# Causal masks of sixteen small heads: from four products of 64x128 to one corner in spare rows and four products of 64x64

## The chip, the cores and the metric

The kernel runs on one core of one Trainium2 chip, in one launch. The metric is the device time in microseconds (us) of that core; the figure compared is the median over several executions. Before the change three executions took 657.17, 661.19 and 665.92 us, so the median is 661.19 us. The profile is of another, single execution, which took 661.49 us; its span from the first to the last instruction of the program is 659.3 us, and the 2.2 us between the two lie around the span.

## The reference, cut to what matters

The input is x of 8 sequences of 512 tokens with 128 features. Two sublayers are added to it, each between layer norms. The first is attention with one wide head of 128. The second starts with attention of 16 heads of width 4 and goes on with a mixture of 8 experts, 2 of which serve a token. The change touches only the 16 small heads:

```python
L, H = (64, 16); HD = L // H                       # 16 heads, 4 wide
h = _rmsnorm(x, g1); c = h @ w_down
q = _rope(split(c @ wq), pos); k = _rope(split(c @ wk), pos); v = split(c @ wv)
scores = jnp.einsum('bhqd,bhkd->bhqk', q, k) / jnp.sqrt(jnp.float32(HD))
causal = jnp.tril(jnp.ones((s, s), bool))          # s = 512 here
scores = jnp.where(causal, scores, -jnp.inf)
attn = jax.nn.softmax(scores, axis=-1)
o = jnp.einsum('bhqk,bhkd->bhqd', attn, v)
```

A query must not see a key behind it. In blocks of 128 queries and 128 keys only the block on the diagonal needs a mask; the blocks above it are left out of the work, and those below it are whole.

## The kernel before, in words

**Stages.** In the first some 120 us the wide attention of all 8 sequences runs (`wide_attention`). From 93 us the small heads run, as 32 units: 8 sequences by 4 groups of 4 heads (`Unit`). From 467 us the experts run (`experts`), and the last results are written.

**How the heads lie.** Each float of a query or a key is split into three bf16 parts, and the products of the parts that matter make 36 rows (`S9`) on the partitions. Two heads, called i = 0 and 1, lie on partitions 0 to 63 and 64 to 127 of `q_rows` and `k_rows` (`HR` is 64). Of the 64 rows of a head, 0 to 35 are the parts, 36 to 61 are zeros, and 62 and 63 (`SM` is 62) are ones in `k_rows` and the negative row maximum in `q_rows`, which L703 writes by DMA. The constant rows are written once, in `fill` (L161), by DMAs from the tile `fixed`.

**A unit.** The scores are computed twice. `rowwise` (L654) puts queries on the partitions, for a block t of 128 queries and the keys up to it, in tile `sm`; `highest` (L674) lets the VectorE (DVE) take the maximum of each row, tile `nm`, L678. `columnwise` (L710) puts keys on the partitions, for a block j of keys and the queries from it on, in tile `sT`; `weights` (L731) lets the ScalarE (ACT) take the exponent, tile `pk`, L741. `weigh` (L743) then multiplies with the values: products of 128 rows and 32 columns, four side by side, into `po`, L748. `sm` and `sT` share three PSUM buffers with everything else that is called "wide", so the TensorE (PE) can start a new group only when DVE or ACT has read the group three before it.

**A group and its masks.** A group is the score products of one or two pairs of heads (L663 in `rowwise`, L718 in `columnwise`: each with 62 or 64 contracted rows and 128 output partitions, for i = 0 and i = 1 in the two halves of the rows) and then the mask, added to the diagonal blocks by `mask` (L642): for each i and for each half h of the block's columns, a product of a 64x128 mask tile with a 64x64 identity adds 0 or -2^100 to all 128 partitions by 64 columns (L646). These are four products for one pair, or four with twice the columns for two pairs. In a unit there are six row groups (four with one pair, two with two) and five column groups (two with one pair, three with two). That makes 352 groups and 1,408 mask products.

**Order.** `period(n)` (L1283) is an order written out by hand: `both` issues a row group of the unit two ahead, then a column group of this unit, then the reductions and exponents of both, and `weigh` products between them. `aside` (L1268) puts pieces of other work between the steps: `ffn_front` and `ffn_back` (projections, transposes) and `route` (the choice of experts). Each engine executes its own instructions in program order. The constant tiles are made on GpSimd (POOL): `mask_q` and `mask_k` by `half_masks` (L436), called from `late_constants` in the first step of the wide attention; `fixed` in `fill`, three steps later.

Of the kernel before, what the change touches and what calls it, by code (L numbers as in the profile page):

```python
# [9 lines left out]
BF16 = mybir.dt.bfloat16  # L10
I32 = mybir.dt.int32
AF = mybir.ActivationFunctionType
ALU = mybir.AluOpType
AX = mybir.AxisListType

P = 128
EPS = 1e-5

NEG_BF = -(2.0**100)
# [3 lines left out]
def kernel(  # L23
# [22 lines left out]
    nc = tc.nc  # L46
    B, T, D = x.shape
    NT = T // P
    L = w_down.shape[1]
    H, HD, HP = 16, 4, 32  # L50
    NG = H // 4
    HR, S9 = P // 2, 9 * HD
    SM = HR - 2
# [8 lines left out]
    const = ctx.enter_context(tc.tile_pool(name="const", bufs=1))  # L62
# [27 lines left out]
    for b in range(B):  # L90
        nc.sync.dma_start(
            out=x_all[:, b * NT : (b + 1) * NT, :],
            in_=x[b].rearrange("(t p) d -> p t d", p=P),
# [33 lines left out]
    for s in range(2):  # L127
# [3 lines left out]
        for c in range(FC):  # L131
            nc.sync.dma_start(
                out=wall[:, es, 2 * F + c * D : 2 * F + (c + 1) * D],
                in_=w2[es, c * P : (c + 1) * P].rearrange("e f d -> f e d"),
# [14 lines left out]
    q_rows, k_rows = [], []  # L149
    for i in range(2):  # L150
        q_rows.append(during.tile([P, H // 2, T], BF16, name=f"q_rows{i}"))
        rows = during.tile([P, H // 2, T], BF16, name=f"k_rows{i}")
# [8 lines left out]
    def fill():  # L161
        for i, pad in enumerate(vpads):
            nc.gpsimd.memset(pad, 0.0)
            nc.gpsimd.memset(pad[:, :, :, i * 2 * HD + HD : i * 2 * HD + HD + 1], 1.0)
            yield
        fixed = const.tile([P // 2, 1, T], BF16, name="fixed")
        nc.gpsimd.memset(fixed[: P // 4], 1.0)
        nc.gpsimd.memset(fixed[P // 4 :], 0.0)
        for rows in k_rows:
            for h in range(2):  # L170
                at = h * HR + SM
                nc.sync.dma_start(
                    out=rows[at : at + 2], in_=fixed[:2].to_broadcast([2, H // 2, T])
                )
        for rows in q_rows + k_rows:
            for h in range(2):
                at = h * HR + S9
                nc.sync.dma_start(
                    out=rows[at : at + SM - S9],
                    in_=fixed[P // 4 : P // 4 + SM - S9].to_broadcast([SM - S9, H // 2, T]),  # L180
                )
        yield

    h_all = keep.tile([P, B * NT, RW], F32, name="h_all")
# [226 lines left out]
    with tc.manual_schedule():  # L411
# [15 lines left out]
        out=mask_a,  # L427
        in_=mask_a,
        compare_op=ALU.is_ge,
        fill=NEG_BF,  # L430
        base=0,
        pattern=[[-1, P]],
        channel_multiplier=1,
    )

    def half_masks(m, sign):  # L436


        nc.gpsimd.memset(m, 0.0)
        for i in range(2):  # L440
            for h in range(2):
                at = m[i * HR : (i + 1) * HR, h, :]
                nc.gpsimd.affine_select(
                    out=at,
                    in_=at,
                    compare_op=ALU.is_ge,
                    fill=NEG_BF,
                    base=sign * HR * h,
                    pattern=[[-sign, P]],
                    channel_multiplier=sign,  # L450
                )

    mask_q = const.tile([P, 2, P], BF16, name="mask_q")
    mask_k = const.tile([P, 2, P], BF16, name="mask_k")
    order = const.tile([P, E], F32, name="order")
    zeros = const.tile([P, RW], F32, name="zeros")
    ones_bf = const.tile([P, P], BF16, name="ones_bf")
# [3 lines left out]
    back_place = const.tile([P, B, 2, NT], I32, name="back_place")  # L461

    def late_constants():
        half_masks(mask_q, -1)
        half_masks(mask_k, 1)
        for e in range(E):
            nc.gpsimd.memset(order[:, e : e + 1], float(E - e))
        nc.gpsimd.memset(zeros, 0.0)
        nc.gpsimd.memset(zeros[:, D : D + 1].bitcast(I32), FAR)
        nc.gpsimd.memset(ones_bf, 1.0)  # L470
        nc.gpsimd.affine_select(
            out=before_me,
            in_=ones_bf,
            compare_op=ALU.is_gt,
            fill=0.0,
            base=0,
            pattern=[[1, P]],
            channel_multiplier=-1,
        )
        nc.gpsimd.memset(upto_me, 1.0)  # L480
        nc.gpsimd.affine_select(
            out=upto_me,
            in_=upto_me,
            compare_op=ALU.is_ge,
            fill=0.0,
            base=0,
            pattern=[[1, E], [-1, E]],
            channel_multiplier=0,
        )
        nc.gpsimd.iota(  # L490
            tile_at,
            pattern=[[P, tile_at.shape[1]]],
            base=0,
            channel_multiplier=0,
            allow_small_or_imprecise_dtypes=True,
        )
        for part in parts:
            part.constants()
# [126 lines left out]
    class Unit:  # L625
# [16 lines left out]
        def mask(self, out, which, i):  # L642

            at = slice(i * HR, (i + 1) * HR)
            for h in range(2):
                nc.tensor.matmul(  # L646
                    out[:, :, h * HR : (h + 1) * HR],
                    which[at, h, :],
                    ident_bf[at, at].unsqueeze(1).to_broadcast([HR, out.shape[1], HR]),
                    start=False,  # L650
                    stop=(h == 1),
                )

        def rowwise(self, t, pairs):  # L654
# [683 lines left out]
    def wide_attention():  # L1338
        for b in range(B + 1):
# [11 lines left out]
            if b == 0:  # L1351
                late_constants()
# [32 lines left out]

    CLOSED = 3
    setup = [prepare(), fill()]
    first = [front_and_rows(0)]
    units_begin = [period(-2), period(-1)]
# [172 lines left out]
```

## Time and profile before

| what | us or share |
|---|---|
| median of three executions | 661.19 |
| the profiled execution, and its span | 661.49, 659.3 |
| stretch of the small heads, 93 to 467 | 374 |
| PE busy in it | 312.69 |
| DVE busy in it; of that the reductions at L678 | 270.91; 194.79 |
| ACT busy in it | 229.71 |
| PE busy with the mask products (L646) in it | 94.54 |
| mean granted TensorE clock, whole span | 0.927 |

A row of groups in the profile gives the line of the kernel, the engine, the operation, the tiles (out<-in), the shape and the count; then the busy time, the mean duration of one, and the idle time before it with what ended it. For PE the shape begins with the rows and columns of the array that the product takes: 64*128 is 64 contracted rows by 128 output partitions, 128*32 is 128 by 32. The moving operand follows: 64x64 bf16 is 64 partitions by 64 columns. PE products are pipelined: a product's duration runs on after the next one has begun, so the busy times of PE say how long something was in flight, and the times from start to start say what a product costs the stream. A timeline merges neighbours of one kind into one line with a count.

### The profile page before, as it was taken

What the parts mean: (1) busy time and instruction counts of PE and PEld (TensorE: products, weight loads), DVE (VectorE), ACT (ScalarE), POOL (GpSimd) and SP (SyncE); (2) the same over time, 40 slices, a digit from 0 to 9 for tenths busy, and PEclk for the clock granted to TensorE, in tenths of its full rate; (3) what the DMA queues carried; (4) which work ended last, traced back from release to release, by engine and by line L of the source; (5) the groups of instructions that cost most, each with busy time, mean ns of one, the idle gap of its engine ahead of it and who ended that gap; (6) DMA issues with size and microseconds to landing.
All of it is one profiled execution on the core that took longest, in us unless ns stands there. A gap on an engine that the chain in (4) does not pass through costs nothing. (4 is left out here: it accounts for less than half of the span.)

```text
span 659.3 us, 14317 instructions
## 1 busy us (share of the span) xinstructions
PE 531.6 (81%) x5098; PEld 313.6 (48%) x5098; DVE 414.7 (63%) x1011; ACT 365.8 (55%) x717; POOL 280.5 (43%) x414
## 2 busy tenths in 40 slices
PE   4999979888989987888989586858889857999810
PEld 2666746544444543434445233424466635666600
DVE  3567846779889888766887474854333514335765
ACT  2656533356768675756776254647755523445642
POOL 3945733122141514653118332050166574555851
PEclk9999989889999999979999597989989987999955
DMA  7741230502312123123241240011411222324453
GB/s 192 199 88 22 60 84 13 134 2 59 90 26 76 49 75 82 51 83 73 54 103 31 66 125 18 3 34 44 106 53 44 73 70 68 83 68 121 127 144 99
DMA packets 65845, 49.36 MB, mean 75 GB/s; under 512 B 10055, under 2 KB 63563, under 8 KB 65776
## 3 DMA queue, kind: packets, MB, share of 16 engines
q1 hardware_dynamic: 58992, 39.03, 23.4%
q0 software_dynamic: 4544, 8.50, 4.0%
q10 hardware_dynamic: 2240, 0.92, 0.5%
q8 instruction: 41, 0.67, 0.4%
q14 instruction: 28, 0.23, 0.1%
HBM read 25.16 MB, written 22.15 MB: 72 GB/s over the span
## 5 line engine op out<-in xcount | busy, mean ns | idle before, releaser
L678 DVE TENSOR_REDUCE nm<-sm 128x2 f32<-128x1024 f32 (+2 forms) x192 | 194.8, 1042 | 57.8 <-PE sm L646 25.2
L741 ACT ACTIVATE pk<-sT 128x1024 f32<-128x1024 f32 x160 | 162.0, 1025 | 98.1 <-PE sT L646 82.5
L814 POOL DMA_INDIRECT answers<-ye_e,xs_e x78 | 78.4, 1006 | 55.8 <-DVE ye_e L1201 37.1
L748 PE MATMUL po<-pk,vpad 128*32 128x512 f32 (+3 forms) x1024 | 100.1, 456 | 2.4 <-ACT foT L933 2.4
L663 PE MATMUL sm<-k_rows,q_rows 62*128 62x256 bf16 (+3 forms) x512 | 73.4, 313 | 23.1 <-DVE nm L678 8.2
L1157 PE MATMUL ph_e<-wall,xT_e 128*128 x156 | 77.7, 621 | 9.0 <-ACT xT_e L1151 7.3
L718 PE MATMUL sT<-q_rows,k_rows 64*128 64x384 bf16 (+3 forms) x512 | 67.0, 309 | 22.0 <-DVE nm L678 11.0
L1169 ACT ACTIVATE sil_e<-ph_e,xs_e 128x256 f32<-128x256 f32 x78 | 32.7, 469 | 68.5 <-PE ph_e L1157 32.2
L1173 DVE TENSOR_TENSOR hid_e<-sil_e,ph_e 128x512 f32<-128x512 f32 (+1 forms) x40 | 27.0, 674 | 60.1 <-ACT sil_e L1169 52.0
L663 PEld LDWEIGHTS <-q_rows 62*128 62x128 bf16 x512 | 25.3, 95 | 72.8 <-issue 66.1
L801 POOL DMA_INDIRECT rows_dram<-h_all,slots x32 | 32.2, 1008 | 60.3 <-DVE slots L1107 52.7
L646 PE MATMUL sm<-ident_bf,mask_q 64*128 64x64 bf16 (+1 forms) x768 | 51.3, 204 | 1.7 <-issue 1.7
L1191 PE MATMUL py_e<-wall,hT_e 128*128 x312 | 44.0, 286 | 7.1 <-DVE ye_e L1201 7.1
L718 PEld LDWEIGHTS <-k_rows 64*128 64x128 bf16 x512 | 24.3, 95 | 51.5 <-issue 48.9
L646 PEld LDWEIGHTS <-mask_q 64*128 64x128 bf16 x768 | 39.9, 98 | 16.4 <-issue 4.1
L646 PE MATMUL sT<-ident_bf,mask_k 64*128 64x128 bf16 (+1 forms) x640 | 44.5, 210 | 0.0
L1191 PEld LDWEIGHTS py_e<-wall,hT_e 128*128 128x128 f32 x312 | 39.8, 199 | 8.2 <-DVE ye_e L1201 7.3
L1201 DVE TENSOR_SCALAR ye_e<-py_e,xs_e 128x128 f32<-128x128 f32 x78 | 23.8, 346 | 30.3 <-PE py_e L1191 12.2
L1157 PEld LDWEIGHTS ph_e<-wall,xT_e 128*128 128x128 f32 x156 | 27.3, 196 | 30.5 <-issue 21.6
L646 PEld LDWEIGHTS <-mask_k 64*128 64x128 bf16 x640 | 31.6, 97 | 12.9 <-issue 1.7
L801 POOL DMA_INDIRECT rows_dram<-rows,slots x32 | 31.1, 972 | 9.8 <-issue 9.2
L286 PE MATMUL pq<-xnT,wqk 128*128 128x512 f32 x64 | 32.1, 628 | 1.8 <-ACT xnT L280 1.2
(205 smaller groups left out, 893.4 us busy)
## 6 DMA issues: line engine op xcount, KB each, us to landing
xs_e<-rows_dram SPq DMA_DIRECT2D x78, 65.5 KB
q_dram<-thirds SPq DMA_DIRECT2D x24, 192.0 KB
k_dram<-thirds SPq DMA_DIRECT2D x24, 192.0 KB
q_rows<-q_dram SPq DMA_DIRECT2D x16, 288.0 KB
k_rows<-k_dram SPq DMA_DIRECT2D x16, 288.0 KB
y<-answers SPq DMA_DIRECT2D x12, 256.0 KB
x_all<-in_L_attn_x_dram SPq DMA_DIRECT2D x8, 256.0 KB
wall<-in_L_ffn_w_dram SPq DMA_DIRECT2D x4, 512.0 KB
```

Of the source, the lines that this page charges most:

```text
L286: nc.tensor.matmul(pq[:, s, :], wqk[:, i, s, :], self.xnT, start=True, stop=True)
L646: nc.tensor.matmul(out[:, :, h * HR : (h + 1) * HR], which[at, h, :], ident_bf[at, at].unsqueeze(1).to_broadcast([HR, out.shape[1], HR]), ...
L663: nc.tensor.matmul(sc[:, i, c * n : (c + 1) * n], self.q[at, 2 * self.g + pair, t * P : n], self.k[at, 2 * self.g + pair, :n], start=(c == 0),
L678: nc.vector.tensor_reduce(self.nm[:, :, pairs[0] : pairs[0] + w, t], sc[:, :, : w * n].rearrange("p i (c n) -> p i c n", n=n), AX.X, ALU.m ...
L718: nc.tensor.matmul(sc[:, i, c : c + n], self.k[at, 2 * self.g + pair, j * P : (j + 1) * P], self.q[at, 2 * self.g + pair, j * P :], start= ...
L741: nc.scalar.activation(p[:, :, :c], sc[:, :, :c], AF.Exp, scale=HD**-0.5)
L748: nc.tensor.matmul(po[h * HP : (h + 1) * HP, j * P :], vpads[self.g][:, j, h, :], self.p[j, h // 2][:, h % 2, :], start=(self.g == 0 and j ...
L801: nc.gpsimd.indirect_dma_start(out=self.rows[:, :], out_offset=bass.IndirectOffsetOnAxis(ap=index, axis=0), in_=src, in_offset=None, bound ...
L814: nc.gpsimd.indirect_dma_start(out=self.answers[:, :], out_offset=bass.IndirectOffsetOnAxis(ap=index, axis=0), in_=src, in_offset=None, bo ...
L1157: nc.tensor.matmul(ph[q][:, i, :], xT[q][:, i * P : (i + 1) * P], part.weights(i0 + i, 0, 2 * F), start=True, stop=True,)
L1169: nc.scalar.activation(sil[:, i], ph[q][:, i, :F], AF.Silu, scale=xs[q][:, i, D + 2 :])
L1191: nc.tensor.matmul(ps[:, i, :], hT[q][:, i, c, :], part.weights(i0 + i, 2 * F + c * D, D), start=(c == 0), stop=(c == FC - 1),)
```

## The change

The mask of a diagonal block of 128 by 128 is taken apart into three corners. The upper right corner, first 64 queries against last 64 keys, is wholly masked: it moves into four of the zero rows of `q_rows` and `k_rows`, one for each block of 128 tokens. Row t of the queries holds 1 at the first 64 tokens of block t, row t of the keys holds -2^100 at its last 64 tokens, so that the score products themselves add -2^100 there. The score products keep their 62 or 64 rows. What is left are the two triangles of 64 by 64 on the diagonal: `mask` adds each by a product of 64 rows by 64 columns into its own quarter, for h = 0 on output partitions 0 to 63 and for h = 1 on 64 to 127. The number of mask products, and the columns that each moves, stay. `mask_q` and `mask_k` shrink to 64 columns; a small tile `marks` is made on POOL in `fill`, and `fill` issues 16 DMAs for the rows 36 to 61 in place of 8. The order of the instructions on PE, DVE and ACT stays the same one by one.

```diff
+        marks = const.tile([NT, 2, T], BF16, name="marks")
+        for k, value in enumerate((1.0, NEG_BF)):
+            nc.gpsimd.memset(marks[:, k], value)
+            for base, sign in ((-HR * k, 1), (HR * (k + 1) - 1, -1)):
+                nc.gpsimd.affine_select(
+                    out=marks[:, k], in_=marks[:, k], compare_op=ALU.is_ge, fill=0.0,
+                    base=base, pattern=[[sign, T]], channel_multiplier=-sign * P,
+                )
-        for rows in q_rows + k_rows:
-            for h in range(2):
-                at = h * HR + S9
-                nc.sync.dma_start(
-                    out=rows[at : at + SM - S9],
-                    in_=fixed[P // 4 : P // 4 + SM - S9].to_broadcast([SM - S9, H // 2, T]),
-                )
+        for k, both in enumerate((q_rows, k_rows)):
+            for rows in both:
+                for h in range(2):
+                    at = h * HR + S9
+                    nc.sync.dma_start(
+                        out=rows[at : at + NT],
+                        in_=marks[:, k : k + 1, :].to_broadcast([NT, H // 2, T]),
+                    )
+                    nc.sync.dma_start(
+                        out=rows[at + NT : h * HR + SM],
+                        in_=fixed[P // 4 : P // 4 + SM - S9 - NT].to_broadcast(
+                            [SM - S9 - NT, H // 2, T]
+                        ),
+                    )
...
-    def half_masks(m, sign):
+    def corner_mask(m, sign):
         nc.gpsimd.memset(m, 0.0)
         for i in range(2):
-            for h in range(2):
-                at = m[i * HR : (i + 1) * HR, h, :]
-                nc.gpsimd.affine_select(
-                    out=at, in_=at, compare_op=ALU.is_ge, fill=NEG_BF,
-                    base=sign * HR * h, pattern=[[-sign, P]], channel_multiplier=sign,
-                )
+            at = m[i * HR : (i + 1) * HR, :]
+            nc.gpsimd.affine_select(
+                out=at, in_=at, compare_op=ALU.is_ge, fill=NEG_BF,
+                base=0, pattern=[[-sign, HR]], channel_multiplier=sign,
+            )
-    mask_q = const.tile([P, 2, P], BF16, name="mask_q")
-    mask_k = const.tile([P, 2, P], BF16, name="mask_k")
+    mask_q = const.tile([P, HR], BF16, name="mask_q")
+    mask_k = const.tile([P, HR], BF16, name="mask_k")
...
             for h in range(2):
+                corner = slice(h * HR, (h + 1) * HR)
                 nc.tensor.matmul(
-                    out[:, :, h * HR : (h + 1) * HR],
-                    which[at, h, :],
+                    out[corner, :, corner],
+                    which[at, :],
                     ident_bf[at, at].unsqueeze(1).to_broadcast([HR, out.shape[1], HR]),
                     start=False,
-                    stop=(h == 1),
+                    stop=True,
                 )
```

More of the change, by code (lines that the diff above doesn't have):

```diff
@@ L174, in fill @@
                 )
-        for rows in q_rows + k_rows:
-            for h in range(2):
-                at = h * HR + S9
-                nc.sync.dma_start(
-                    out=rows[at : at + SM - S9],
-                    in_=fixed[P // 4 : P // 4 + SM - S9].to_broadcast([SM - S9, H // 2, T]),
-                )
+        marks = const.tile([NT, 2, T], BF16, name="marks")
[3 more added lines that the diff above has]
+                nc.gpsimd.affine_select(
+                    out=marks[:, k],
+                    in_=marks[:, k],
+                    compare_op=ALU.is_ge,
+                    fill=0.0,
+                    base=base,
+                    pattern=[[sign, T]],
+                    channel_multiplier=-sign * P,
+                )
+        for k, both in enumerate((q_rows, k_rows)):
[12 more added lines that the diff above has]
+                    )
         yield
@@ L434 @@
     )
-    def half_masks(m, sign):
+    def corner_mask(m, sign):
         nc.gpsimd.memset(m, 0.0)
         for i in range(2):
-            for h in range(2):
-                at = m[i * HR : (i + 1) * HR, h, :]
-                nc.gpsimd.affine_select(
[L444 to L450, printed above, removed]
-                )
-    mask_q = const.tile([P, 2, P], BF16, name="mask_q")
-    mask_k = const.tile([P, 2, P], BF16, name="mask_k")
+            at = m[i * HR : (i + 1) * HR, :]
+            nc.gpsimd.affine_select(
+                out=at,
+                in_=at,
+                compare_op=ALU.is_ge,
+                fill=NEG_BF,
+                base=0,
+                pattern=[[-sign, HR]],
+                channel_multiplier=sign,
+            )
+    mask_q = const.tile([P, HR], BF16, name="mask_q")
+    mask_k = const.tile([P, HR], BF16, name="mask_k")
     order = const.tile([P, E], F32, name="order")
@@ L463, in late_constants @@
     def late_constants():
-        half_masks(mask_q, -1)
-        half_masks(mask_k, 1)
+        corner_mask(mask_q, -1)
+        corner_mask(mask_k, 1)
         for e in range(E):
```

## The prediction

> **What bounds the kernel now.** I read the page's busy shares and slices first, then one stretch from 93 to 467 us, where all the mask products lie, then who waits for whom in it, and last single groups in the timeline. From the page:
>
> ```profile
> PE 531.6 (81%) x5098; PEld 313.6 (48%) x5098; DVE 414.7 (63%) x1011; ACT 365.8 (55%) x717; POOL 280.5 (43%) x414
> ...
> PE   4999979888989987888989586858889857999810
> DVE  3567846779889888766887474854333514335765
> ```
>
> From the table of stretches (columns: length; busy us and count of PE, weight loads, DVE, ACT, POOL; clock; DMA) and from the waits of that stretch (us in total, times, longest):
>
> ```profile
> 93.00:467.00 374.00, 312.69 (x3965) 168.60 (x3964) 270.91 (x534) 229.71 (x384) 118.75 (x177) 0.94 0.23 58
> ...
> PE sT L718 <- DVE nm L678: 11.0, 20, 1.1
> PE sm L663 <- DVE nm L678: 8.2, 18, 2.2
> PE sm L663 <- ACT pk L741: 6.9, 13, 2.4
> PE sT L718 <- ACT pk L741: 4.5, 4, 2.0
> ...
> ACT pk L741 <- PE sT L646: 82.5, 90, 6.9
> DVE nm L678 <- PE sm L646: 25.2, 37, 3.8
> ```
>
> PE is the fullest engine at 84% of the stretch, but DVE has 72%, and PE waits 30.6 us for buffers that DVE or ACT must read first. Of the 352 groups a consumer stands idle for at least 127 (90 + 37). So PE and its readers take turns. I followed the releases back from the last `po` product at 466.9 us, as the page's chain does from the end: of 374 us PE has 184, DVE 123, ACT 24, and 182 of 372 runs of mask records (some groups are split by waits) lie on the chain: half.
>
> What a mask costs is not its 191 to 224 ns of duration, but the time until the next product starts. Timeline (start, length):
>
> ```profile
> 301.07 0.22 PE L646 MATMUL sm<-ident_bf,mask_q 64*128 64x64 bf16 x4
> 301.23 0.23 PE L695 MATMUL m3T_ps<-ident_bf,m 128*32 128x128 bf16 x1
> ...
> 303.48 0.22 PE L646 MATMUL sm<-ident_bf,mask_q 64*128 64x64 bf16 x4
> 303.54 0.38 PE L718 MATMUL sT<-q_rows,k_rows 64*128 64x512 bf16 x2
> 303.75 0.22 PE L646 MATMUL sT<-ident_bf,mask_k 64*128 64x64 bf16 x4
> 303.90 0.43 PE L748 MATMUL po<-pk,vpad 128*32 128x128 f32 x8
> ...
> 309.91 0.29 PE L646 MATMUL sT<-ident_bf,mask_k 64*128 64x128 bf16 x4
> 310.13 0.64 PE L748 MATMUL po<-pk,vpad 128*32 128x256 f32 x8
> ```
>
> Four mask products of 64 columns, followed by a product of the same shape (64*128), take 0.06 us of the stream (303.48 to 303.54). Followed by another shape they take 0.16 (301.07 to 301.23) or 0.15. A change of shape thus costs 0.09 to 0.10 us. The single records agree: from start to start 117 against 26 ns after 64 bf16 columns, 525 against 429 after 512 f32 columns. It doesn't take a change of rows: a 128*32 product of 128 f32 columns is followed by a 128*128 one after 203 ns, where 110 is the step without a change. With 128 columns the masks take 0.22 less one change, 0.12. All masks together: 192 groups x 0.06 + 160 x 0.12 = 30.7 us of stream, not the 94.5 us of busy time.
>
> **The change, part by part.** (1) *Masks in 64*64 instead of 64*128.* In the order of the built program every group now goes from 64*128 to 64*64 (352 changes), and 168 of them go back to 64*128 afterwards; the other 184 were followed by another shape already. The changes of shape rise from 402 to 922, by 520. No row shows 64*128 to 64*64. From below: nothing, since two neighbours named 128*128 and 128*64 cost nothing (112 and 109 ns at 478.8 and 479.2 us, where 110 is the plain step). From above: 98 ns, the dearest ordinary change (128*32 to 64*128). I take 93 ns, because in the built program those 128*64 transposes carry no column group and so are no change, while the new masks carry one, as 128*32 does. 520 x 0.093 = 48.4 us.
>
> (2) *Four quarters at once.* Products of 128*32 start 7 ns apart and run side by side; if quarters do that, a group takes 27 ns of columns (53 for two pairs; 64 and 128 columns at the 0.42 ns that 512 columns in 215 ns give) + 3 x 7 + the weights. The weights can no longer be loaded ahead of the change: 27 ns uncovered for 128*32 f32 (454 from one round of four to the next, for 427 of columns) and 11 for 64*128 bf16 (226 against 215); 64 bf16 columns lie between, or at twice 27 at worst; I take 20. That is 68 and 94 ns against 62 and 118: 192 x 6 - 160 x 24 = -2.7 us. Ends: -17 us (27 and 53 ns with nothing else) and +9 (weights 54).
>
> (3) *Weights after the 168 returns:* 168 x 11 ns = 1.8 us, by the 64*128 row, between 0 and 4.5 (27 ns each).
>
> (4) *Score products:* same rows, columns and count: nothing. DVE and ACT do the same.
>
> (5) *Setup.* POOL makes `marks` after `fixed`, at 36.8 us: two memsets at the 0.51 of `fixed` and four selects of 512 elements, between 0.29 (128 elements, L443) and 1.14 (four times that); at 0.75, 4.0 us together. POOL is idle for 1.64 us before `roped` at 38.40, again for 0.52 us, and after 42.6 us, so the second `roped`, done at 41.46, slips to about 43.3; the scores that read it start at 43.34. Cost 0 to 1 us. If that cover were gone, at most the 4.0. The smaller masks save some 1.5 us on POOL at 18 to 21 us, which can be worth that or nothing; together I put 0. SP issues 8 more DMAs of about 1 us each (L178: 3.85 for four) and starts them up to 4 us later, so it ends near 61 instead of 48.9; what is queued behind is the first `q_dram` store, at 74.42.
>
> Sum on PE: 48.4 - 2.7 + 1.8 = **+47.5 us** of stream in 374 us.
>
> **How much reaches the end.** At most all of it. At least what lies on the chain: half of the entries, (32.7 - 2.7) x 0.49 = 14.7, and 79 of 188 returns by the records, 17.4 x 0.42 = 7.3: 22 us. Each group that becomes later pulls the chain over to PE, so the truth lies between; what hides the rest is DVE's queue of reductions (194.8 us at L678), and without that cover it is 47.5. I take +33, a little under the middle. What is late next is the reader: `nm` and `pk` wait longer for their groups, and the 30.6 us that PE waits for buffers shrink. The experts after 467 us only start later. From the profiled execution 661.49 + 33 = 694.5; the median is 0.3 lower: **694 us**.
>
> The Trainium skill, in "TensorEngine Tiling (Array Packing)", section "Tiling Modes", says that a change of the tiling mode, not of the tile, makes TensorE run empty; the 0.09 to 0.10 us above agree with it, but it has no figure for them. The same page, under "Theoretical Speedup", gives twofold for a small output dimension; by that alone the 30.7 us would halve, an estimate of -15 us, or 646. The section "Gotcha 2: Feature Incompatibilities" there rules out the fast weight load with column tiling, which speaks for the dearer end of (2); no row shows 64 bf16 columns.
>
> **The rivals.** *A: a change between 64*128 and 64*64 costs nothing.* The rows keep their halves, only the columns split in two, and the only changes seen that cost are to or from quarters of the columns or of the row split. For it: the two 128*64 neighbours. Against: 128*32 to 128*128. Price: weights are then loaded ahead, groups take 48 and 74 ns against 62 and 118, 192 x 14 + 160 x 44 = 9.7 us less stream, two thirds of it at the end: 655 us, not slower. It decides below 19 ns a change (520 x 0.019 = 9.7). With the -17 of (2), all on the path, 644.
>
> *B: paid, but hidden.* DVE is busy when 155 of 192 groups arrive, by the waits; if its queue covers two thirds and more of the 47.5, the time is 661.5 + 12 = 673 or less. Against it: 90 of 160 exponents find ACT idle, and the chain's half is a floor.
>
> *C: more than the sum.* Seven pieces of the stretch, 48 us of 374, run at a granted clock of 0.5; there a change costs twice: 520 x 48/374 x 0.093 = 6 us more. With all of the sum on the path: 715. Above that, if the thinner stream is granted the full clock less often.
>
> **How the numbers follow.** Forecast, the changes paid and half to wholly on the path: 0.79, 675 to 715. A: 0.08, of which 0.03 under 648. B: 0.08, 661 to 674. C beyond 716: 0.05. The range 670 to 716 takes in the forecast and the upper part of B, some 8 in 10. This kernel's three runs differ by 1.3%, so under 2% nothing can be told: faster by over 2% (under 648) 0.03, within 2% (to 674.4) 0.13, slower 0.84.
>
> **What would show it.** Masks as 64*64; from the start of the scores to the masks 0.09 us more than the columns take (0.21 at 303.54 to 0.31); from the masks to a score product 0.15 to 0.18 us instead of 0.06; busy time of L646 lower though the stretch is longer; more idle time of DVE and ACT before `nm` and `pk`; POOL and SP unchanged after 75 us. Steps of 0.21 and 0.05 instead would prove A. I am wrong in the price if the stretch grows by over 50 us, in the landing if the steps are as said and it grows by under 15.

## The result

The changed kernel takes 687.61 us (median of four executions, 686.91 to 689.59), the kernel before 659.18 (four, the three named above among them, 654.85 to 665.92): 1.042 times as long, with a 95% interval of 1.037 to 1.047, or 28 us more. The forecast was 694 in a range of 670 to 716. The profiled execution took 686.91 us with a span of 684.8, which is 25.5 us more than the span before.

From the page of the kernel after: busy time of each engine, the busy tenths of PE and DVE in 40 slices, and the shares of the chain that ended last.

```profile
PE 574.3 (84%) x5098; PEld 304.7 (44%) x5098; DVE 417.1 (61%) x1011; ACT 369.2 (54%) x717; POOL 283.1 (41%) x416
...
PE   5999979799999998979989885987979986999910
DVE  3577836768778787756688473676133443434865
...
PE 66%; DVE 14%; ACT 6%; DMA 4%; issue 3%; another core or an unknown queue 3%; POOL 2%; SPq 1%; ACTq 0%; POOLq 0%; DVEq 0%
```

PE is fuller and DVE emptier than before, with as many instructions on each. From the stretch of the small heads, now 93 to 497 us: its row in the table of stretches (columns as before the change), the same for the mask products alone (L666 is the old L646), and the waits (us in total, times, longest).

```profile
93.00:497.00 404.00, 358.03 (x3972) 161.06 (x3970) 272.38 (x536) 233.29 (x386) 118.77 (x177) 0.91 0.21 54
...
93.00:497.00 404.00, 85.70 (x1408) 40.76 (x1408) 0.91 0.21 54
```

```profile
ACT pk L761 <- PE sT L666: 106.9, 103, 5.0
DVE nm L698 <- PE sm L666: 51.7, 57, 4.9
PE sT L738 <- DVE nm L698: 13.2, 24, 4.4
...
PE sm L683 <- ACT pk L761: 5.2, 12, 1.5
...
PE sT L738 <- ACT pk L761: 3.8, 3, 2.6
...
PE sm L683 <- DVE nm L698: 2.1, 4, 0.7
```

The mask products are in flight for less time than before (85.7 against 94.5 us), and yet the stretch is 28 us longer. The readers wait more for the masks: ACT 106.9 us against 82.5, DVE 51.7 against 25.2. PE waits less for buffers: 13.2 + 5.2 + 3.8 + 2.1 = 24.3 us against 30.6. From the first score product to the first transpose of the experts it was 375.7 us (91.6 to 467.2); now it is 403.8 (92.5 to 496.3). So the whole loss lies here; the experts behind it took 192.1 us to the end of the span and now take 188.5, by instructions that the change does not touch, and why they take less is not known.

The timeline of the changed kernel (start, length), at the same place in the order as the lines shown before the change:

```profile
318.49 0.39 PE L683 MATMUL sm<-k_rows,q_rows 62*128 62x512 bf16 x2
318.81 0.22 PE L666 MATMUL sm<-ident_bf,mask_q 64*64 64x64 bf16 x4
318.96 0.23 PE L715 MATMUL m3T_ps<-ident_bf,m 128*32 128x128 bf16 x1
...
321.04 0.34 PE L683 MATMUL sm<-k_rows,q_rows 62*128 62x384 bf16 x2
321.30 0.22 PE L666 MATMUL sm<-ident_bf,mask_q 64*64 64x64 bf16 x4
321.46 0.39 PE L738 MATMUL sT<-q_rows,k_rows 64*128 64x512 bf16 x2
321.78 0.22 PE L666 MATMUL sT<-ident_bf,mask_k 64*64 64x64 bf16 x4
321.93 0.42 PE L768 MATMUL po<-pk,vpad 128*32 128x128 f32 x8
```

From the scores to their masks it is 0.32 us after 512 columns (318.49 to 318.81, 321.46 to 321.78), where it was 0.21 (303.54 to 303.75). From the masks to scores it is 0.16 us (321.30 to 321.46), where it was 0.06. From the masks to a product of another shape it is 0.15 us, as before. The two steps that grew are those at which a change of shape was added.

### The profile page after: what moved, and what is told of

It is laid out like the page before. It is cut to its first block, busy times and chain, and to the rows that moved or that the text cites. A ratio compares the mean times of both kernels' runs of the same rounds, so it can differ in the third digit from the quotient of the medians.

```text
span 684.8 us, 14324 instructions
## 1 busy us (share of the span) xinstructions
PE 574.3 (84%) x5098; PEld 304.7 (44%) x5098; DVE 417.1 (61%) x1011; ACT 369.2 (54%) x717; POOL 283.1 (41%) x416
## 4 chain that ended last, share of the span: by engine, by line
PE 66%; DVE 14%; ACT 6%; DMA 4%; issue 3%; another core or an unknown queue 3%; POOL 2%; SPq 1%; ACTq 0%; POOLq 0%; DVEq 0%
PE po L768 12%; PE ph_e L1177 10%; PE sT L738 7%; PE sm L683 6%; DVE nm L698 6%; PE py_e L1211 5%; PE sm L666 4%; PE sT L666 4%; PE pqk L597 2%; PE pq L306 2%; PE ht_e L1200 2%; ACT pk L761 1%; PE pu L983 1%; PE pr L371 1%
## 5 line engine op out<-in xcount | busy, mean ns | idle before, releaser
L698 DVE TENSOR_REDUCE nm<-sm 128x2 f32<-128x1024 f32 (+2 forms) x192 | 195.1, 1044 | 77.6 <-PE sm L666 51.7
L761 ACT ACTIVATE pk<-sT 128x1024 f32<-128x1024 f32 x160 | 163.5, 1026 | 126.5 <-PE sT L666 106.9
L768 PE MATMUL po<-pk,vpad 128*32 128x512 f32 (+3 forms) x1024 | 102.4, 478 | 1.6 <-ACT foT L953 1.6
L834 POOL DMA_INDIRECT answers<-ye_e,xs_e x78 | 78.9, 1011 | 51.7 <-DVE ye_e L1221 35.0
L738 PE MATMUL sT<-q_rows,k_rows 64*128 64x384 bf16 (+3 forms) x512 | 68.3, 321 | 23.5 <-DVE nm L698 13.2
L1177 PE MATMUL ph_e<-wall,xT_e 128*128 x156 | 76.1, 610 | 8.0 <-issue 4.1
L683 PEld LDWEIGHTS <-q_rows 62*128 62x128 bf16 x512 | 22.1, 94 | 65.0 <-issue 54.7
L666 PE MATMUL sm<-ident_bf,mask_q 64*64 64x64 bf16 (+1 forms) x768 | 45.8, 227 | 0.4 <-issue 0.4
L738 PEld LDWEIGHTS <-k_rows 64*128 64x128 bf16 x512 | 20.7, 95 | 54.1 <-issue 43.6
L666 PEld LDWEIGHTS <-mask_q 64*64 64x64 bf16 x768 | 22.2, 105 | 41.8 <-issue 38.8
L666 PE MATMUL sT<-ident_bf,mask_k 64*64 64x128 bf16 (+1 forms) x640 | 39.9, 236 | 0.8 <-issue 0.8
L666 PEld LDWEIGHTS <-mask_k 64*64 64x64 bf16 x640 | 18.6, 105 | 39.9 <-issue 39.8
```

The lines of the kernel that those rows point to most:

```text
L666: nc.tensor.matmul(out[corner, :, corner], which[at, :], ident_bf[at, at].unsqueeze(1).to_broadcast([HR, out.shape[1], HR]), start=False, ...
L683: nc.tensor.matmul(sc[:, i, c * n : (c + 1) * n], self.q[at, 2 * self.g + pair, t * P : n], self.k[at, 2 * self.g + pair, :n], start=(c == 0),
L698: nc.vector.tensor_reduce(self.nm[:, :, pairs[0] : pairs[0] + w, t], sc[:, :, : w * n].rearrange("p i (c n) -> p i c n", n=n), AX.X, ALU.m ...
L738: nc.tensor.matmul(sc[:, i, c : c + n], self.k[at, 2 * self.g + pair, j * P : (j + 1) * P], self.q[at, 2 * self.g + pair, j * P :], start= ...
L761: nc.scalar.activation(p[:, :, :c], sc[:, :, :c], AF.Exp, scale=HD**-0.5)
L768: nc.tensor.matmul(po[h * HP : (h + 1) * HP, j * P :], vpads[self.g][:, j, h, :], self.p[j, h // 2][:, h % 2, :], start=(self.g == 0 and j ...
```

## The experiments

The runs were made on several chips. On two of them the kernel before takes 609 to 610 us, on a third 660. Every ratio below is to the kernel before on the same chip; the us follow from ratio and that time. In short diffs, "-" is the kernel named in the sentence ahead of it, and "..." stands for lines that are left out.

### The rows alone

The changed kernel with the masks of the kernel before: the corner rows and all their setup stay (`marks` lies in a working tile here), the mask products and their mask tiles are 64x128 again.

```diff
...
-                    out[corner, :, corner],
-                    which[at, :],
+                    out[:, :, h * HR : (h + 1) * HR],
+                    which[at, h, :],
...
```

> The corner rows and their setup as after the change, but the masks as before it: two 64x128 products for each i. No change of shape is added (402 as before). Theory 'changes of shape': nothing of the 27 us is left, 0.995 to 1.01 of the kernel before. Rival 'rows and setup' (marks on GpSimd, 8 more DMAs, rows that are no longer zero): most of the 27 us stays, 1.03 or more.

Measured: 1.0007 (0.998 to 1.003). The marks on GpSimd, the 8 additional DMAs, and rows that hold marks instead of zeros cost nothing that can be told (the interval reaches 1.5 us to either side).

### The quarters alone

The kernel before with the 64x64 masks, but without the corner rows; so the upper right corner of each diagonal block is left unmasked.

```diff
...
-                    out[:, :, h * HR : (h + 1) * HR],
-                    which[at, h, :],
+                    out[corner, :, corner],
+                    which[at, :],
...
```

> The masks as after the change (64x64 products, 922 changes of shape), but the rows 36 to 61 all zero as before it; the masking of the upper right corner of each diagonal block is left out. Theory 'changes of shape': the whole loss is here, 1.035 to 1.05 of the kernel before. Rival 'rows and setup': 1.00 to 1.01.

Measured: 1.0445 (1.039 to 1.050), 27 us. The whole loss is in the shape of the mask products.

### The price of a change of shape by itself

The kernel before with one small product between the scores and the masks of each group. It adds zeros, moves 16 columns, and has 64 output columns in the one run and 128 in the other:

```diff
+            nc.tensor.matmul(
+                sc[:64, 0, :16], no_mask[:HR, :64], ident_bf[:HR, :16],   # or [:128] and [:HR, :128]
+                start=False, stop=False,
+            )
```

> The kernel before, with one small product of 64 rows by 64 columns and 16 moving columns, which adds zeros, between the scores and the masks of each group: 352 products, 704 more changes of shape (352 there, 352 back). Theory 'changes of shape', at 0.09 us each and some 0.03 us for the weights: 352 x 0.21 = 74 us of stream, of which 60 to 90% reach the end, 44 to 67 us: 1.065 to 1.10. Rival 'the quarters and their weights are slow, not the change': 352 x 0.03 to 0.05 = 11 to 18 us of stream, 1.01 to 1.03.

> The same with the small product at 64 rows by 128 columns, the shape of its neighbours: 352 products, no more changes of shape. Theory 'changes of shape': 352 x 0.01 to 0.03 = 4 to 10 us of stream, 1.00 to 1.01. Rival 'any extra product between scores and masks costs so much': as much as with 64x64, 1.06 or more.

Measured: 1.087 (1.083 to 1.091) with 64x64, 53 us; 1.005 (1.003 to 1.008) with 64x128, 3 us. The timeline of the 64x64 run (the small product is L658, the masks L648):

```profile
300.59 0.39 PE L675 MATMUL sm<-k_rows,q_rows 62*128 62x512 bf16 x2
300.91 0.19 PE L658 MATMUL sm<-ident_bf,no_mask 64*64 64x16 bf16 x1
301.04 0.23 PE L648 MATMUL sm<-ident_bf,mask_q 64*128 64x64 bf16 x4
301.11 0.39 PE L731 MATMUL sT<-q_rows,k_rows 64*128 64x256 bf16 x4
```

And of the 64x128 run:

```profile
300.45 0.34 PE L675 MATMUL sm<-k_rows,q_rows 62*128 62x384 bf16 x2
300.63 0.17 PE L658 MATMUL sm<-ident_bf,no_mask 64*128 64x16 bf16 x1
300.63 0.24 PE L648 MATMUL sm<-ident_bf,mask_q 64*128 64x64 bf16 x4
```

With 64x64 the product of 16 columns (7 ns at 0.42 ns each) holds the stream for 0.13 us until the masks, and the masks of four products behind it take 0.07, where it was 0.06. With 64x128 it vanishes between its neighbours. In the single records 347 of the 352 steps from it to the masks are 125 or 126 ns: 7 for the columns, 92 or 93 for the change as on the way in, and some 26 left, which are put down to weights that could not be loaded ahead; no run separates these from the change. So it is neither the number of products nor their columns, but the change of shape: 704 more changes, 352 x 0.22 = 77 us of stream, of which 53 reach the end, 69%. The granted clock plays no part in this one: the profiled execution has 10 us at half clock in the stretch of the small heads, as the run with the rows alone has.

### Fewer changes of shape by another order

The changed kernel with the scores of the row group and of the column group first, and the masks of both behind them:

```diff
...
-                v.rowwise(t, pairs)
+                late.append(v.rowwise(t, pairs))      # scores now, masks later
             for job in between:
                 job()
             if unit:
-                unit.columnwise(parts)
+                late.append(unit.columnwise(parts))
+            for masks in late:
+                masks()
```

> The kernel after the change, but in each call of both the scores of the row group and of the column group come first and the masks of the two last, so that the 64x64 products stand together: 653 changes of shape instead of 922 (402 before the change). Theory 'changes of shape': 251 more than before at 0.09 us = 23 us, less 5 us for the narrower masks of groups with two pairs, times 0.6 = 11 us: 1.01 to 1.025 of the kernel before. Rival 'the 64x64 products themselves are slow': as after the change, 1.04. It can also be slower than the sum says, because the row maxima wait for the column scores too.

Measured: 1.088 (1.083 to 1.093), twice the loss of the change itself. Both theories missed it. The warning at the end of the expectation names what the waits show (`nm` is L702 here, `sT` L742, `pk` L769):

```profile
ACT pk L769 <- PE sT L666: 115.0, 128, 4.0
DVE nm L702 <- PE sT L666: 53.2, 78, 1.9
PE sT L742 <- ACT pk L769: 24.6, 29, 1.0
DVE nm L702 <- PE sm L666: 21.3, 25, 4.3
PE sT L742 <- DVE nm L702: 18.5, 29, 0.8
```

DVE now waits 53.2 us until the column masks are through (0.5 in the run with the rows alone), and PE waits 43.1 us (24.6 + 18.5) for a buffer before the column scores, with the row masks held up behind it. The same order with the masks and the rows of the kernel before separates order and shape.

> The order of the run with the masks together (scores of the row group and of the column group first, then the masks of the two), but with the 64x128 masks and the rows of the kernel before: no change of shape is added (402). Theory 'the order cost that run its gain: the row maxima and the buffers wait for the column scores': this order alone costs 30 to 45 us, 1.05 to 1.075 of the kernel before. Rival '64x64 products that stand together are slow in a way of their own': 1.00 to 1.02.

Measured: 1.061 (1.053 to 1.069), 40 us, without one more change of shape. So the order alone costs 6.1%. If the two losses add up, 2.7% are left for the 251 changes that the first run has above the kernel before, 16 us with some 6 either way, as the two runs were made on different chips; the sum in the expectation had 11 for them. Both runs had a lower granted clock than the kernel before (0.923 to 0.935 against 0.954 to 0.970, and 0.894 to 0.916 against a median of 0.934), so a part of both losses goes with the clock.

### What hides the rest

Two runs, before and after, in which DVE takes the maximum over the first half of the keys only, with the scale of the exponents at 0.05; both give another output than the reference.

```diff
-                sc[:, :, : w * n].rearrange("p i (c n) -> p i c n", n=n),
+                sc[:, :, : w * n].rearrange("p i (c n) -> p i c n", n=n)[:, :, :, : n // 2],
...
-            nc.scalar.activation(p[:, :, :c], sc[:, :, :c], AF.Exp, scale=HD**-0.5)
+            nc.scalar.activation(p[:, :, :c], sc[:, :, :c], AF.Exp, scale=0.05)
```

> The kernel before, with the VectorE taking each row maximum over the first half of the keys only, and the scale of the exponents set to 0.05 so that nothing overflows: the reductions lose some 80 of 195 us of the VectorE's time, and the output is another one. It is the base for the next run. If half of the chain ran through the VectorE, as read from the trace before, 0.93 to 0.97 of the kernel before; if the TensorE alone bounded, 0.99 to 1.00.

> The kernel after the change with the same halved maxima and the same scale of the exponents as the run before it. Theory 'the queue of reductions hides the rest of the 44 us': with a lighter VectorE more of the stream reaches the end, 34 to 44 us above the run before it (0.055 to 0.07 in the ratio). Rival 'it is hidden elsewhere (ScalarE, copies, DMA)': the same 25 to 28 us as with the whole maxima.

Measured: 0.961 (0.957 to 0.965) for the kernel before with halved maxima, 1.013 (1.008 to 1.019) for the kernel after. A row of the groups of each (the kernel before first: busy time, mean ns, idle before):

```profile
L678 DVE TENSOR_REDUCE nm<-sm 128x2 f32<-128x512 f32 (+2 forms) x192 | 112.4, 600 | 73.7 <-PE sm L646 71.5 <-PE sT L646 1.2
```

```profile
L698 DVE TENSOR_REDUCE nm<-sm 128x2 f32<-128x512 f32 (+2 forms) x192 | 113.2, 601 | 100.5 <-PE sm L666 99.6 <-issue 0.7
```

82 us less of DVE (194.8 to 112.4) bring 24 us, so DVE did carry a part of the path before. The change of the masks now costs 0.052 of 609.9, 32 us, against the 27 of the quarters with whole maxima. That lies between what the two theories expected (34 to 44, and 25 to 28), and with the intervals of the ratios (some 4 us each way on the difference) it is not far enough from 27 to be called shown. (The clocks of these two runs hardly differ, while some 5 of the 27 us go with a lower clock, as estimated below; so the gap may be larger.) DVE's reductions are also only lighter here, not gone. So these runs do not say how much of the stream DVE's queue hides, nor what hides the rest.

### Taking changes of shape out of the kernel before

The kernel before has 402 changes; many stand around the value products (`weigh`, 128*32). First run: three of four calls next to the transpose of the maxima, which has their shape.

```diff
-        weigh(0)
         yield
         both(3, C, None, None)
         if nxt:
             nxt.turn_m()
+        for j in (0, 3, 1):
+            weigh(j)
...
-        weigh(3)
...
-        both(2, C, u, ((0, 1),), [lambda: weigh(1)])
+        both(2, C, u, ((0, 1),))
```

> The kernel before with three of the four weigh calls of a unit moved next to the transpose of the maxima, which has their shape of 128x32: 164 fewer changes of shape (238 instead of 402), nothing else left out. Theory 'changes of shape': 164 x 0.093 = 15 us of stream less, 60% of it at the end: 9 us, 0.98 to 0.99 of the kernel before. Rival 'the order matters more': a longer run of value products keeps the readers of the scores waiting, 1.00 to 1.02.

Measured: 1.006 (1.003 to 1.009). Then two smaller moves. `weigh(1)` directly behind `weigh(3)`, which stands at the end of the step before:

```diff
         weigh(3)
+        weigh(1)
...
-        both(2, C, u, ((0, 1),), [lambda: weigh(1)])
+        both(2, C, u, ((0, 1),))
```

> The kernel before with one value product call (block 1) moved to stand behind another (block 3), before the row scores of the next step instead of between row and column scores: 58 fewer changes of shape (344 instead of 402). 58 x 0.093 = 5.4 us of stream. Theory 'a saved change is worth its price': 0.990 to 0.997 of the kernel before. Rival 'value products between a row and a column group give the readers time, and the change is hidden there': 1.000 to 1.006.

Measured: 1.0001 (0.997 to 1.004). And `weigh(3)` down to `weigh(1)`, between the row and the column scores:

```diff
-        weigh(3)
...
-        both(2, C, u, ((0, 1),), [lambda: weigh(1)])
+        both(2, C, u, ((0, 1),), [lambda: weigh(3), lambda: weigh(1)])
```

> The same two calls side by side, but between the row scores and the column scores of the later step: 50 fewer changes of shape (352 instead of 402), 4.7 us of stream. Theory 'a saved change is worth its price': 0.990 to 0.997. Rival 'the order matters more': the step that loses its call now has row and column scores back to back and waits for buffers, 1.000 to 1.006.

Measured: 1.008 (1.004 to 1.011). 164, 58 and 50 fewer changes bring nothing or a small loss. The waits of PE for buffers in the first of the three runs:

```profile
PE sT L718 <- DVE nm L678: 23.9, 45, 1.6
...
PE sm L663 <- DVE nm L678: 4.2, 8, 1.1
PE sm L663 <- ACT pk L741: 3.5, 11, 0.7
...
PE sT L718 <- ACT pk L741: 2.6, 5, 0.9
```

On a chip of the same speed the run with the rows alone, whose PE stream is that of the kernel before, waits 13.7 us in 21 places for `nm` before the column scores; here it is 23.9 in 45. In the kernel before, on a chip of the speed of the two smaller runs, the same wait is 11.0 us in 20 places; with `weigh(1)` behind `weigh(3)` it is

```profile
PE sT L718 <- DVE nm L678: 24.0, 39, 4.5
```

All of PE's waits for `nm` and `pk` before scores come to 36.9 us there and to 40.9 in the run with both calls between the scores, against 30.6 in the kernel before. That is 6 and 10 us more, where the saved changes were worth 5.4 and 4.7. So, by these waits, the order gave back what the changes saved: the value products between a row and a column group had filled time in which DVE reads a buffer. That their changes of shape stood in that time as well fits this, but no run shows it by itself. In the run with 164 fewer changes the waits grew by 8 us, which does not make up for 15. Its granted clock was lower as well (0.944 to 0.961 against 0.954 to 0.970); what else took the rest is open. None of the three runs is faster than the kernel before.

## Why the prediction was right

**The step that decided, the price of a change of shape, was right**, although no row of the trace before showed 64*128 to 64*64. The records after show the steps 146, 199, 263 and 316 ns from 128, 256, 384 and 512 columns of scores to the masks; less 53, 107, 160 and 213 for the columns, and less 11 for weights where a group has only one score product on each half (the last two), that is 92 or 93 each time, where 93 was taken. The number, 520, comes from the order of the program and could not miss; counted in the records of the two traces it is 520 as well. Rival A (a change that costs nothing) is out. Why the two 128*64 neighbours cost nothing was put down to transposes that carry no column group; that fits, but no run tests it.

**The quarters** do run side by side, and are cheaper than put: they start 3 ns apart, not 7. From the last of four products of 64 columns to another shape it is 143 ns: 27 of columns, 92 of the change, so 24 are left for weights, where 20 was taken. A group takes 9 + 24 + 27 = 60 ns with one pair and 9 + 24 + 53 = 86 with two, against the 68 and 94 of the prediction and the 62 and 118 of the kernel before: 192 x 2 + 160 x 32 = 5.5 us saved, where 2.7 was put. The twofold that the prediction quotes from the Trainium skill ("TensorEngine Tiling (Array Packing)", "Theoretical Speedup") is "Up to 2×" on that page; 62 to 60 and 118 to 86 ns is what came of it here, before the two changes of shape are added.

**The sum** of the stream is then 520 x 0.092 + 1.8 - 5.5 = 44 us, against 47.5. Group by group, from the first score product to the product behind the masks, the records at full clock come to the same 44 us.

**What reaches the end** is 28.1 of 44 us, 64%, where 33 of 47.5, 69%, was taken: inside the bounds of 22 and all of it, and nearer the floor. The 33 was a choice between these bounds, not worked out, so its nearness to 28 is in part luck. Following the releases back from the last value product of the changed kernel, PE has 294 of 404 us of the chain and DVE 61, where it was 184 and 123 of 374; 258 of 352 groups lie on it, where it was half. So the chain moved over to PE as forecast. That this is why more than the floor arrived is a reading; with it go the 69% of the probe, a larger dose, whose chain has 308 us of PE and 53 of DVE, against 174 and 131 in the run with the rows alone.

A part of the 28 us goes with the clock, not with the stream alone. Of the stretch 75 us ran at half clock after the change and 48 before; with the quarters alone it was 31 us, with the rows alone 10. In the executions of the kernel before, on each of the three chips, each us more at half clock (from the granted clock of each execution) went with 0.2 to 0.25 us more time. So some 5 of the 28 us, and of the 27 of the quarters, go with the lower clock, an estimate from these figures. The landing of the stream itself is then nearer to the floor of 22 than to the 33 taken.

**The setup** cost 0: `roped` was done at 42.9 us instead of 41.5, before the scores that read it, and SP finished the rows at 58.4 us, well ahead of the store at 74.5. The run with the rows alone confirms it.

**Rival B** (paid, but hidden by DVE) is out for the kernel as it is; the runs with halved maxima leave open how much of the 36% that did not arrive is due to DVE. **Rival C** (more than the sum) did not come as a time. Its reason was half wrong: a change does not cost twice at half clock. There the step from 512 columns to the masks is 536 ns instead of 316, and from 256 columns 347 instead of 199; the columns take 427 and 213, so 109 are left where it was 103, and 134 where it was 92. The other half, less full clock, did come: the granted clock of the stretch fell from 0.94 to 0.91, and with the quarters alone it was lower than in the kernel before in nearly every execution (0.942 to 0.954 against 0.953 to 0.970). Why is not known; with the probe, which adds more changes, it did not fall (0.957 to 0.970).

## What to carry to other kernels

Price a small product on TensorE by the step from its start to the start of what follows, not by its busy time: the masks were 94.5 us busy and 31 us of stream, so there was little to win. A new array shape between two products of another one cost the change twice here (0.09 us each) and some 0.03 us more. The reverse does not follow: taking changes of shape out by another order gained nothing in three runs, and in two of them PE's longer waits for its buffers account for it.

## What was not expected of the hardware

Products of 64x64 in four quarters start 3 ns apart, those of 128x32 in four strips 7 ns apart.

The same kernel took 609 to 610 us on two chips and 659 to 661 on two occasions elsewhere. In the profiled run with the rows alone (span 607.4 us), whose PE stream is that of the kernel before, the stretch of the small heads had a mean granted clock of 0.99 and took 342 us from the first score product to the first transpose of the experts; in the kernel before (span 659.3 us) it was 0.94 and 375.7. Half clock filled 48 us of the stretch in the kernel before and 10 in the other, which accounts for at most 19 us of the 33. Of the rest, 11.9 us are three waits of DVE before `nm` that the profile puts to another core or an unknown queue; the run with the rows alone has none of them. What caused them, and what the remainder is, stays open. The loss by the 64x64 masks was the same on both within its interval, 1.042 and 1.045.
